# A four-layer sequence model on one core: the sorting's memory pool is opened ahead of the attention's weights, and the last element's scatters and expert tiles are given out from the second half sequence on

## The chip, the core and the metric

The kernel runs on one core of a Trainium2 chip. Such a core has five engines with an instruction queue each: TensorE (PE, matrix products), VectorE (DVE), ScalarE (ACT), GpSimd (POOL) and SyncE (SP, which here only issues DMAs). The metric is the device time of one execution in microseconds; the time of a kernel is the median of its runs.

## The reference, cut to what matters

Input x has 4 batch elements of 1024 tokens with 128 features. Four layers of two sublayers each are applied, and every sublayer is followed by `layernorm(x + sublayer(x))`. The change touches the border between the second sublayer of layer 2 and the first of layer 3, so these and their neighbours matter:

```python
x = norm(x + L2_attn(x))   # causal linear (cosformer) attention, 16 heads of 64
# L2_ffn: 8 experts, the best 2 of each token
probs = softmax(x @ router_w.T); weights, indices = top_k(probs, 2)
y = (silu(x @ w13[..., :256]) * (x @ w13[..., 256:])) @ w2      # per expert
x = norm(x + sum over the 2 chosen of weight * y)
# L3_attn: a Mamba block, 256 channels, 16 states
h = exp(delta * A) * h + delta * x * B_t ; y_t = sum over the states of h * C_t
x = norm(x + ...)
# L3_ffn: 8 experts, all computed, gated by a top-p mask
x = norm(x + sum over the 8 of gate * (relu(x @ W1 + b1) @ W2 + b2))
```

Everything is in float32.

## The kernel before, in words

The kernel is written in a framework that takes a traced program, gives each instruction a priority by its place in the program, and lets a planner order the instructions of each engine at compile time: when an engine is free in the planner's own account of time, it gets the ready instruction of the highest priority. So the order in the program is a wish, and the order on each engine is fixed once compiled. Within a pool, tiles of the same name share a number of buffers. Pools are opened and closed like a stack, on the left or the right side of on-chip memory; a pool that lies on memory of a closed pool waits for that pool's last accesses.

The parts of the program are Python generators that are stepped in turn.

- The cosformer attention (`l2_attn`) goes through 128 units: 4 batch elements x 4 quarters of 256 tokens x 8 head pairs. Its work tiles are in the pool `cos` (left), its weights in `w2` (right). The order of PE's instructions is the program's own there.
- After the last quarter of an element, `l2_dispatch` routes its 1024 tokens and sorts them by expert: it counts on DVE (its tiles are in the pool `moed`), then yields "put" and gives out 16 scatters on POOL (L1410, `xrows<-xN,di`), each of 128 token rows into a DRAM buffer. The destinations `di` and weights `wt` are in another pool, `moek`.
- `l2_ffn` is one generator, called `moe` where it is stepped. It runs over 92 tiles, 23 for each of the 4 elements, in a software pipeline: rows are loaded 8 tiles ahead (`xg`, L1469), the tile's expert weights 4 ahead (`wx`, L1485), then come the two products (`ph` or `pa_m<-xgT,wx` and `py<-wx,mh`). Before it takes up a tile whose element has not all its scatters given out, the whole pipeline is held with empty steps. When an element's last tile is through, `l2_combine` gathers the two results of each token with 16 gathers on POOL (L1556, `yg<-yrows,di`), adds and norms.
- For the last element (3) the attention's loop has ended when its sorting is done, so its 16 scatters remain as the generator `rest`.
- `l3` goes through 8 half sequences ("halves", 512 tokens each; halves 0 and 1 are element 0). Each half has a preparation (`l3_prepare`), a scan over the 16 states (`l3_scan`), and a finish. For each state, SP loads two rows broadcast to all partitions (`bn`, `cn`, L1871), POOL multiplies (`db`, L1876), ACT takes an exponential (`da`, L1880), DVE scans (L1881), POOL multiplies again (`hc`, L1892) and PE sums over the states (`pys`). For elements 1 to 3 a part of the sums is done by an accumulating DMA from POOL's queue. Half 0 is prepared during the attention, in the pool `first` and in memory that is free there. `l3` opens the pools `ssm` and `ssm2` on the left; bn, cn, db and hc are tiles of `ssm2`, with 4 buffers each.
- Between the states, `l3` gives out: a step of `rest`, a step of `moe` (two in half 0), and 3 or 4 steps of `work`, the final MoE (`l3_experts`) of earlier halves, whose weights `wh` and hidden tiles `hh` (L2007) are in the pool `top` (right). The scan's instructions are traced with a raised priority.

On the right side, pools are opened in this order: `moek`, `first`, `moet` (the tiles of `l2_ffn`), `w2`, then `moed`; `w2` and `moed` close after the attention, and `top` opens in their place.

Of the kernel before, what the change touches and what calls it, by code (L numbers as in the profile page):

```python
# [19 lines left out]
B, T, D = 4, 1024, 128  # L20
# [31 lines left out]
def weave(*gens):  # L52

    gens = list(gens)
    while gens:
        for g in gens[:]:
            if next(g, gens) is gens:
                gens.remove(g)
# [13 lines left out]
class Net:  # L72
# [1355 lines left out]

    def l2_ffn(self, wp):

        units = [
            dict(st=st, j=j, n=min(4, NT2 - j // 4 * 4))
            for st in self.m2["st"]
            for j in range(NT2)
        ]
        n = len(units)
        side = []
        for t in range(-8, n + 4):  # L1440
            while t + 8 < n and "put" not in units[max(t + 8, 0)]["st"]:
                for g in side[:]:
                    if next(g, self) is self:
                        side.remove(g)
                yield
            if 0 <= t + 8 < n and units[t + 8]["j"] % 4 == 0:
                self.l2_load_rows(units[t + 8], units, t + 8, wp)
            if 0 <= t + 4 < n:
                self.l2_weights(units[t + 4], wp)
            if 0 <= t + 2 < n:  # L1450
                self.l2_load_tile(units[t + 2], units, t + 2, wp)
            if 0 <= t < n:
                self.l2_hidden(units[t], wp)
            if 0 <= t - 2 < n:
                u = units[t - 2]
                self.l2_expert_out(u, units, t - 2, wp)
                if u["j"] == NT2 - 1:
                    side.append(self.l2_combine(u["st"], wp))
            for g in side * 2:
                if next(g, self) is self and g in side:  # L1460
                    side.remove(g)
            yield
        for g in side:
            yield from g
# [157 lines left out]
    def l3(self, moe, fp):  # L1622

        c3 = self.c3
        halves = [dict(b=b, h=h) for b in range(B) for h in range(2)]
        for i, u in enumerate(halves):
            u["prev"] = halves[i - 1] if u["h"] else None  # L1630
        halves[0] = dict(self.c3["first"], **{k: halves[0][k] for k in ("prev",)})
        for i, u in enumerate(halves[1:], 1):
            u["prev"] = halves[i - 1] if u["h"] else None
        work = self.l3_experts(fp)
        end = iter(())
        for i, u in enumerate(halves):
            nxt = iter(())
            if i + 1 < len(halves):
                if halves[i + 1]["h"] == 0:
                    while "done" not in self.m2["st"][halves[i + 1]["b"]]:  # L1640
                        next(moe)
                nxt = self.l3_prepare(halves[i + 1])
            u["final"] = i + 1 == len(halves)
            scan = self.l3_scan(u)
            for n in range(NST):
                with self.tc.high_priority(offset=1000):
                    next(scan)
                    next(end, None)
                    next(nxt, None)
                for k in range(1):  # L1650
                    next(self.m2["rest"], None)
                next(moe, None)
                if i == 0:
                    for k in range(1):
                        next(moe, None)
                for k in range(4 if n % 8 == 7 else 3):
                    next(work)
                for v in c3["todo"]:
                    v["age"] += 1
            for f in chain(scan, end, nxt):  # L1660
                pass
            end = chain(self.l3_sum(u), self.l3_finish(u))
        for f in end:
            next(work)
        c3["all"] = True
        for f in work:
            pass
# [530 lines left out]
def program(tc, io):  # L2198
    with ExitStack() as ctx:
        n = Net(ctx, tc, io)  # L2200
        wd, w0 = ExitStack(), ExitStack()
        wdp = wd.enter_context(tc.tile_pool(name="wd", bufs=1))
        W = n.l0_load(w0.enter_context(tc.tile_pool(name="w0", bufs=1)))
        d = n.l1_ffn_load(wdp)
        dp = ctx.enter_context(
            tc.tile_pool(name="rows", bufs=2, space=bass.MemoryType.DRAM)
        )
        sd = ctx.enter_context(tc.tile_pool(name="ssmd", bufs=2, space=bass.MemoryType.DRAM))
        with ExitStack() as ff:
            last = n.front(ff, w0, W, d, dp)  # L2210
            keep = ctx.enter_context(tc.tile_pool(name="moek", bufs=1, side="right"))
            first = ctx.enter_context(tc.tile_pool(name="first", bufs=1, side="right"))
            mt = ctx.enter_context(tc.tile_pool(name="moet", bufs=2, side="right"))
            w2 = ExitStack()
            n.l2_attn_load(w2.enter_context(tc.tile_pool(name="w2", bufs=1, side="right")))
            weave(*last)
        wd.close()
        def load():
            n.l2_ffn_load()
            n.l3_load(sd)  # L2220
            n.l2_rows(keep, md, dp)

        moe = n.l2_ffn(mt)
        with w2:
            md = w2.enter_context(tc.tile_pool(name="moed", bufs=1, side="right"))
            n.l2_attn(load, n.l2_dispatch, moe, first)
        n.l3_pools(ctx)
        fp = ctx.enter_context(tc.tile_pool(name="top", bufs=2, side="right"))
        n.l3(moe, fp)
# [17 lines left out]
```

## Time and profile before

| | before |
|---|---|
| runs, median (lowest to highest) | 2261.67 us (2253.73 to 2262.74), 3 runs |
| the profiled execution: time, span | 2265.2 us, 2263.4 us |
| mean granted TensorE clock | 0.934 |
| PE, DVE, ACT, POOL busy | 1988.1, 1361.8, 1184.6, 1025.0 us |
| busy in the attention's last stretch, 1200 to 1297 us: PE, DVE, POOL | 83.40, 53.87, 35.58 of 97.00 us |
| first and last scatter of element 3 issued | 1344.8, 1366.1 us |
| first and last product `db` of the scans | 1363.5, 2110.7 us |
| first matmul of the final MoE | 1525.2 us |
| after the last scan, 2126.8 to the end: PE busy | 124.30 of 136.60 us |

The span runs from the first to the last instruction of the profiled execution; its time is a little longer. Times of events below are from the span's start. A busy PE need not be PE at its peak, since matmuls are pipelined, and "granted clock" is the share of full speed at which TensorE ran.

### The profile page before, as it was taken

What the parts mean: (1) busy time and instruction counts of PE and PEld (TensorE: products, weight loads), DVE (VectorE), ACT (ScalarE), POOL (GpSimd) and SP (SyncE); (2) the same over time, 40 slices, a digit from 0 to 9 for tenths busy, and PEclk for the clock granted to TensorE, in tenths of its full rate; (3) what the DMA queues carried; (4) which work ended last, traced back from release to release, by engine and by line L of the source; (5) the groups of instructions that cost most, each with busy time, mean ns of one, the idle gap of its engine ahead of it and who ended that gap; (6) DMA issues with size and microseconds to landing.
All of it is one profiled execution on the core that took longest, in us unless ns stands there. A gap on an engine that the chain in (4) does not pass through costs nothing.

```text
span 2263.4 us, 46328 instructions
## 1 busy us (share of the span) xinstructions
PE 1988.1 (88%) x17791; PEld 1392.3 (62%) x17791; DVE 1361.8 (60%) x3705; ACT 1184.6 (52%) x2578; POOL 1025.0 (45%) x813
## 2 busy tenths in 40 slices
PE   6778889899999999999979866688898999999998
PEld 3565555544577777787768654356565656565666
DVE  7767644433455654754555555696877688686522
ACT  6532434322344444454555556476768787676443
POOL 5100411000123244234143339989788889789400
PEclk9778979889999999999999987799999999999999
DMA  3010110050000000031222066466776676676421
GB/s 107 0 38 10 31 38 1 23 172 0 2 3 2 14 27 22 25 91 41 78 79 81 17 193 193 127 193 191 205 209 172 185 186 190 181 203 170 113 61 52
DMA packets 138605, 211.04 MB, mean 93 GB/s; under 512 B 18645, under 2 KB 75982, under 8 KB 137999
## 3 DMA queue, kind: packets, MB, share of 16 engines
q1 hardware_dynamic: 126238, 173.81, 25.4%
q0 software_dynamic: 12144, 34.26, 7.3%
q8 instruction: 140, 2.29, 0.4%
q14 instruction: 83, 0.67, 0.1%
HBM read 160.22 MB, written 23.16 MB: 81 GB/s over the span
## 4 chain that ended last, share of the span: by engine, by line
PE 44%; DVE 13%; ACT 10%; issue 3%; DMA 2%; POOL 1%; SPq 0%; DVEq 0%; ACTq 0%; POOLq 0%
PE py L140 8%; PE ph L140 7%; PE po L1153 5%; DVE db L1881 5%; PE pa_m L140 5%; PE pqk L140 5%; PE kp_mo L140 3%; PE pr L1223 2%; PE pys L140 2%; PE pv L140 2%; PE pt L144 1%; ACT da L1880 1%; ACT hh L2007 1%; PE kp_mo L144 1%; ACT xN L187 1%
## 5 line engine op out<-in xcount | busy, mean ns | idle before, releaser
L1086 POOL TENSOR_TENSOR qt<-r_q,sb_c_turn 128x256 f32<-128x256 f32 (+1 forms) x256 | 164.7, 664 | 451.0 <-ACT r_q L1078 447.1
L1892 POOL TENSOR_TENSOR hc<-db,cn 128x1024 f32<-128x1024 f32 x128 | 319.0, 2529 | 67.4 <-PE pys L140 26.8
L140 PEld LDWEIGHTS py<-wh,hh 128*128 128x128 f32 x2048 | 257.0, 196 | 79.8 <-issue 47.8
L1876 POOL TENSOR_TENSOR db<-ud,bn 128x1024 f32<-128x1024 f32 x112 | 293.1, 2679 | 7.6 <-ACT dl L1841 5.1
L140 PE MATMUL ph<-xT,wh 128*128 128x512 f32 x512 | 252.9, 611 | 24.0 <-ACT hh L2007 6.7
L140 PE MATMUL py<-wh,hh 128*128 128x128 f32 x2048 | 263.8, 280 | 10.8 <-ACT hh L2007 4.2
L2007 ACT ACTIVATE hh<-ph,sb_cols 128x512 f32<-128x512 f32 x256 | 170.3, 681 | 118.3 <-PE ph L140 92.1
L1144 DVE TENSOR_TENSOR a<-pa_m,sb_c_near 128x256 f32<-128x256 f32 x256 | 96.7, 419 | 201.4 <-PE pa_m L140 201.4
L1101 ACT ACTIVATE kN<-kp_mo,sb_c_trig 128x128 f32<-128x128 f32 x448 | 130.2, 372 | 130.6 <-PE kp_mo L144 122.4
L1880 ACT ACTIVATE da<-dl,aneg 128x512 f32<-128x512 f32 x224 | 153.6, 689 | 74.4 <-DVE db L1881 73.7
L140 PE MATMUL pys<-hc,sb_c_ident 128*128 128x512 f32 x324 | 160.6, 625 | 21.3 <-POOL hc L1892 17.9
L1881 DVE TENSOR_TENSOR_SCAN db<-da,carry,db 128x512 f32<-128x512 f32 x128 | 156.9, 1265 | 21.5 <-POOL db L1876 11.2
L1881 DVE TENSOR_TENSOR_SCAN db<-da,db 128x512 f32<-128x512 f32 x128 | 149.4, 1206 | 11.5 <-ACT da L1880 6.4
L140 PEld LDWEIGHTS ph<-xT,wh 128*128 128x128 f32 x512 | 88.0, 194 | 104.3 <-issue 49.0
L2032 DVE SCALAR_TENSOR_TENSOR h_acc<-py,gt,h_acc 128x128 f32<-128x128 f32 x252 | 70.8, 343 | 123.7 <-PE py L140 123.7
L140 PE MATMUL pqk<-xT,wE 128*128 128x256 f32 x512 | 136.4, 389 | 8.2 <-ACT coT L1220 4.2
L140 PEld LDWEIGHTS pys<-hc,sb_c_ident 128*128 128x128 f32 x324 | 61.1, 201 | 83.8 <-issue 57.7
L140 PEld LDWEIGHTS pqk<-xT,wE 128*128 128x128 f32 x512 | 88.5, 193 | 21.9 <-DVE cv L1063 8.1
L1220 ACT COPY coT<-pt 128x512 f32<-128x512 f32 x64 | 37.5, 587 | 116.8 <-PE pt L144 116.8
L140 PE MATMUL po<-ht,wD 128*128 128x512 f32 x192 | 92.9, 594 | 0.0
L1153 PE MATMUL po<-cv,a 128*64 128x65 f32 x2048 | 88.3, 228 | 0.0
L1556 POOL DMA_INDIRECT yg<-yrows,di x64 | 61.3, 957 | 57.5 <-DVE ch L1388 36.7
(463 smaller groups left out, 4255.2 us busy)
## 6 DMA issues: line engine op xcount, KB each, us to landing
wx<-in_wF SPq DMA_DIRECT2D x92, 384.0 KB, 3.4
bn<-rows SPq DMA_DIRECT2D x128, 256.0 KB, 4.7
cn<-rows SPq DMA_DIRECT2D x128, 256.0 KB, 4.2
wh<-in_wH SPq DMA_DIRECT2D x64, 512.0 KB, 3.8
hc<-hc POOLq DMA_DIRECT2D x47, 512.0 KB, 7.0
xrows<-zero SPq DMA_DIRECT2D x4, 1472.0 KB, 12.0
xg<-xrows SPq DMA_DIRECT2D x20, 256.0 KB, 3.6
yrows<-ys SPq DMA_DIRECT2D x20, 256.0 KB, 3.4
```

The lines of the kernel that those rows point to most:

```text
L140: return self.nc.tensor.matmul(out=out, lhsT=lhsT, rhs=rhs, start=start, stop=stop)
L1086: nc.gpsimd.tensor_mul(u["qt"][:, m, a:], u["q"][:, a:], c2["turn"][:, m, o + a : o + 2 * P])
L1101: self.nc.scalar.activation(u["kN"][:, c, m, :], pk[:, c, :], AF.Copy, scale=trig[:, k, m : m + 1])
L1144: nc.vector.tensor_mul(u["a"][:, i, :, :], pa[i], self.c2["near"][:, None, :].to_broadcast([P, 2, P]),)
L1153: self.nc.tensor.matmul(out=u["po"][self.HALF[j], i, c, :], lhsT=lhsT, rhs=rhs, start=key not in u["begun"], stop=True, skip_group_check=True,
L1556: nc.gpsimd.indirect_dma_start(out=yg[h][:, k, c, :], out_offset=None, in_=st["out"][:, :], in_offset=bass.IndirectOffsetOnAxis(ap=st["des ...
L1876: nc.gpsimd.tensor_mul(db, ud, bc[0])
L1880: nc.scalar.activation(da, dl[:, ec, :], AF.Exp, scale=aneg[:, j : j + 1])
L1881: nc.vector.tensor_tensor_scan(db[:, ec, :], da, db[:, ec, :], carry[:, ec, n : n + 1] if h else 0.0, ALU.mult, ALU.add,)
L1892: nc.gpsimd.tensor_mul(hc, db, bc[1])
L2007: nc.scalar.activation(ht, ph, AF.Relu, bias=self.col("h_b1", i=e * NK + k))
L2032: nc.vector.scalar_tensor_tensor(acc[:, c, :], py[:, c, :], gt[:, c, e : e + 1], acc[:, c, :], ALU.mult, ALU.add,)
```

## The change

It has two parts. The pool `moed` is opened before `w2` and not after it, so that on the right side it lies next to `moet`; both still close together after the attention. And `l2_ffn` now goes through its tiles in two pipelines, one for elements 0 to 2 (69 tiles) and then one for element 3 (23 tiles), so that only the second one is held for element 3's scatters; these are given out one per state in halves from the second on, no longer in the first. The step that drains `moe` before a new element's first half tolerates its end.

```diff
--- before.py
+++ after.py
@@ -1428,11 +1428,14 @@
 
     def l2_ffn(self, wp):
 
-
+        yield from self.l2_tiles_of(0, B - 1, wp)
+        yield from self.l2_tiles_of(B - 1, B, wp)
+
+    def l2_tiles_of(self, b0, b1, wp):
 
         units = [
             dict(st=st, j=j, n=min(4, NT2 - j // 4 * 4))
-            for st in self.m2["st"]
+            for st in self.m2["st"][b0:b1]
             for j in range(NT2)
         ]
         n = len(units)
@@ -1638,7 +1641,7 @@
             if i + 1 < len(halves):
                 if halves[i + 1]["h"] == 0:
                     while "done" not in self.m2["st"][halves[i + 1]["b"]]:
-                        next(moe)
+                        next(moe, None)
                 nxt = self.l3_prepare(halves[i + 1])
             u["final"] = i + 1 == len(halves)
             scan = self.l3_scan(u)
@@ -1647,7 +1650,7 @@
                     next(scan)
                     next(end, None)
                     next(nxt, None)
-                for k in range(1):
+                if i:
                     next(self.m2["rest"], None)
                 next(moe, None)
                 if i == 0:
@@ -2212,6 +2215,7 @@
             first = ctx.enter_context(tc.tile_pool(name="first", bufs=1, side="right"))
             mt = ctx.enter_context(tc.tile_pool(name="moet", bufs=2, side="right"))
             w2 = ExitStack()
+            md = w2.enter_context(tc.tile_pool(name="moed", bufs=1, side="right"))
             n.l2_attn_load(w2.enter_context(tc.tile_pool(name="w2", bufs=1, side="right")))
             weave(*last)
         wd.close()
@@ -2222,7 +2226,6 @@
 
         moe = n.l2_ffn(mt)
         with w2:
-            md = w2.enter_context(tc.tile_pool(name="moed", bufs=1, side="right"))
             n.l2_attn(load, n.l2_dispatch, moe, first)
         n.l3_pools(ctx)
         fp = ctx.enter_context(tc.tile_pool(name="top", bufs=2, side="right"))
```

## Prediction

> **What bounds the kernel now.** I read the page first (engine shares, slices), then a table by stage, then the instruction timelines of SP, VectorE (DVE), ScalarE (ACT) and GpSimd (POOL) around the hand-over from the cosformer attention to the Mamba block, since both edits land there. The page says that TensorE (PE) carries the kernel and that POOL is heavy in the last 40%:
>
> ```profile
> PE 1988.1 (88%) x17791; PEld 1392.3 (62%) x17791; DVE 1361.8 (60%) x3705; ACT 1184.6 (52%) x2578; POOL 1025.0 (45%) x813
> PE   6778889899999999999979866688898999999998
> POOL 5100411000123244234143339989788889789400
> PEclk9778979889999999999999987799999999999999
> ```
>
> From slice 26 on (1471 us) PE is near 90% to the end. In the three slices before it, 1301 to 1471, it has its hole: 60%, and the granted clock falls with it. The table by stage (span, then busy PE, PEld, DVE, ACT, POOL, then clock, DMA share, GB/s) cuts that hole:
>
> ```profile
> 1318.00:1345.00 27.00, 16.19 (x104) 15.09 (x104) 15.72 (x70) 13.15 (x38) 7.88 (x9) 0.82 0.57 157
> 1345.00:1363.50 18.50, 5.89 (x30) 4.54 (x31) 7.68 (x22) 9.15 (x19) 14.23 (x15) 0.68 0.88 316
> 1363.50:1452.30 88.80, 59.45 (x188) 32.95 (x189) 57.45 (x81) 52.77 (x113) 82.62 (x43) 0.78 0.51 152
> 1452.30:1526.00 73.70, 59.92 (x259) 38.69 (x258) 65.15 (x112) 47.66 (x94) 67.04 (x33) 0.91 0.57 174
> ```
>
> PE is busy 16.19 + 5.89 + 59.45 + 59.92 = 141.5 of 208 us: 66.5 us idle. In half 0 (1363.5 to 1452.3) POOL is busy 82.6 of 88.8: the scan's two multiplications per state, on POOL, are the bound. The hole ends at 1525.15, when PE gets its first matmul of the final MoE (ph<-xT,wh); that needs half 0 scanned, normed and routed.
>
> Now who starts the scan. The timelines (start, us, engine, line, what; idle before and its releaser in brackets):
>
> ```profile
> 1317.47 1.12 DVE L191 TENSOR_SCALAR xN<-cr,ln_mv,ln_rs 128x128 f32<-128x128 f32 x4
> 1319.34 0.31 ACT L1754 ACTIVATE sq<-xN 128x128 f32<-128x128 f32 x1
> 1344.50 0.24 DVE L1404 TENSOR_TENSOR wt<-wt,sm 128x8 f32<-128x8 f32 x2
> 1344.82 0.33 SPq L1871 DMA_DIRECT2D bn<-rows  x1
> 1334.69 1.00 POOL L1556 DMA_INDIRECT yg<-yrows,di  x1 [36.74 <-DVE ch L1388]
> 1344.77 0.99 POOL L1410 DMA_INDIRECT xrows<-xN,di  x1 [0.30 <-DVE wt L1404]
> 1363.52 2.37 POOL L1876 TENSOR_TENSOR db<-xT,bn 128x1024 f32<-128x1024 f32 x1
> 1366.06 1.00 POOL L1410 DMA_INDIRECT xrows<-xN,di  x1 [0.17 <-issue]
> 1374.24 0.99 POOL L1556 DMA_INDIRECT yg<-yrows,di  x1 [0.16 <-DVE xc L1792]
> ```
>
> The scan's row loads (bn) go out 0.1 us after the last read of `sm`, a tile of the sorting's pool (`moed`), though the rows were written at 1270.76 and their operand at 1297. The pool `ssm2`, with bn, lies on memory of `moed` and waits for the whole of it. `ssm`, which doesn't, begins with sq at 1319.34, as soon as the attention's last read of its own pool (xN<-cr, until 1318.6) is over. Then POOL serves 15 of element 3's 16 scatters before its first multiplication.
>
> **The pool.** `top`, opened next to `moet` after the attention, holds 3 x 4 + 6 x 2 + 2 x 2 + 2 = 30 KB per partition, `moed` about 9 (two 2 KB router tiles and small ones): with `moed` opened first, it lies wholly under `top`, and `ssm2` meets only the pools of the attention and its weights, both read for the last time by 1318.6. So bn goes out at about 1319.3 instead of 1344.8 and lands 4.7 us later (its median): first multiplication possible at 1324. `top` (wh, hh) now waits for the sorting, about 1345 or, with the scan's DVE work mixed in, 1360; its first use is 140 us later: nothing, unless a wh load stands on SP ahead of bn loads and holds them; at most the 4 states loaded ahead, 4 x 4.7 = 19 us, are cover. The earlier position moves the attention's weights by 9 KB; they are loaded at 451 and first read at 585.8: nothing, and 130 us of cover.
>
> **The scatters.** 16 at 1.27 us from start to start (0.97 + 0.30) = 20.3 us leave the place before the scan and go to half 1, one per state. The first multiplication moves from 1363.5 to 1324: 39.5 us. Something is late next. Eight gathers of element 1 (1334.69 to 1344.5, 10 us), which ran on an idle POOL, now lie inside half 0: 29.5 left. Element 2's tiles are no longer held for element 3's scatters, so its first eight gathers (1520 before; 10 us) may fall in half 0 too; counting steps, they are given out at state 12 of 16. I take half: 25 us, bounds 19.5 and 29.5. So half 0 ends near 1427 and the final MoE starts near 1500 instead of 1525.
>
> **What PE pays.** PE's time is saved only where it idled. Four of element 3's 23 tiles ran in the hole (1504 to 1520); all 23 now come in halves 2 and 3, by the step count, where PE had no idle time over 3.4 us. A tile is 1.13 + 0.61 us: 4 x 1.74 = 7.0 us. In half 1 the scatters slow the scan: some 11 of 16 before 1500, 14 us of POOL, 3 states, whose sums (1.88 us each on PE) move behind: 5.6 us. Half 1 is otherwise POOL-bound as before, 67.0 of 73.7. Element 3's results are gathered in half 4 instead of 3 and needed before half 6: nothing. Sum: 25 - 7.0 - 5.6 = 12.4 us. The profiled execution took 2265.2 us (span 2263.4), 3.5 above the median of 2261.67: 2265.2 - 12.4 = 2252.8, and on the median 2249.
>
> One rule speaks against half 1. Half 0 ran at a granted clock of 0.78 with gaps of 9.5 and 5.8 us before sums; half 1 at 0.91 with element 2's and 3's tiles as filler. In half 1 no such tiles remain, so I leave PE's durations there as in half 0, which the 66.5 us already contain. The Trainium skill, "TensorE: Matmul & The Clock Gate" (Why this matters for your kernels), says that an idle gap over some 3 us drops the clock to half; by that alone the sums of half 1, some 19 us at full speed, would take up to twice as long, an estimate from the page, and the gain would be nearly nothing.
>
> **The rivals.**
> (a) POOL gives it all back: no change. From 1334.7 to half 2's first multiplication at 1539.5 POOL is rarely idle: 30.5 us of gathers, 20.3 of scatters, about 31 x 2 x 2.35 = 146 of products, 197 of 205. The same work started at 1324 ends 10.7 us earlier at best, and if element 2's last eight gathers (1549) come forward, 0.7 us. If halves 1 and 2 rather than the start of the final MoE set PE's work, the gain is 0 to 10 us: 2252 to 2262. For it: the sum. Against: after 1539 PE, not POOL, is the fuller engine.
> (b) Slower: the planner, which placed all 16 scatters into the first POOL gap, though one is given out per state, puts them in half 0 again, between products, as soon as their indices exist. Half 0 then holds 20.3 us more; with element 2's gathers the start moves 19.5 - 20.3: nothing gained, and element 3's tiles still stand in program order behind half 1: the 7.0 us and up to 7 more tiles' worth of crowding in halves 2 and 3 (12.2 us) are lost. Between +8 and +20; I take +12, 2274 on the median. It decides once more than 25 - 12.6 = 12 us of scatters slip into half 0. Against: products are given a higher priority and POOL had only 3.6 us of gaps inside half 0.
> (c) More: scatters and gathers fall into POOL's gaps of halves 2 to 4 (it is busy 87.5 of 103.9 us in half 2), half 0 shifts the full 29.5, and nothing is lost on PE: 2232.
> (d) The change misses: bn still waits, for another tile of the sorting or the load queue, and only the scatters go: 1363.5 to about 1350, 13 us, less 12.6: no change, 2262.
>
> **How the numbers follow.** A measurement of this kernel can tell about 0.5%, 11 us, from no change; 2249 lies just beyond it. My sum with its bounds and (c) get 0.56 together, of which some 0.05 lie within 11 us; (a) and (d) 0.25, of which 0.03 beyond it; (b) 0.19, nearly all beyond. So faster 0.54, same 0.28, slower 0.18. The range reaches from a little under (c), since waits on wx loads (19.8 us in the hole, with DMA at 316 GB/s while scan rows, wh and wx load together) may also shrink, to just short of (b): 2228 to 2271.
>
> **What would show it.** Right: bn issued near 1319, not after the last read of `sm`; the first product near 1324; no scatter before it; the final MoE's first matmul near 1500; half 2 beginning at 1530 to 1540; PE idle in the hole near 54 us. Wrong: scatters between products of half 0 (rival b); a final MoE that starts early while PE in half 1 is under 60% busy and halves 2 and 3 take longer than 104 and 113 us (a); bn after 1340 (d). If the time differs while everything up to the first product is as told, my account of PE is wrong.

## The result: 40 us slower, and the profile after

| | before | after |
|---|---|---|
| median of the runs | 2262.2 us (2253.73 to 2266.24, 4 runs) | 2302.4 us (2300.59 to 2303.98, 4 runs) |
| ratio, 95% interval | | 1.0179 [1.0159, 1.0199] |
| span and clock of the profiled execution | 2263.4 us, 0.934 | 2299.7 us, 0.926 |

The forecast was 2249 us, with a range up to 2271. The page of the changed kernel, engine shares and slices, against the first fence of the prediction:

```profile
PE 2001.6 (87%) x17791; PEld 1400.2 (61%) x17791; DVE 1374.2 (60%) x3705; ACT 1181.0 (51%) x2574; POOL 1025.7 (45%) x813
...
PE   6778889899899999999879866679898989898998
...
POOL 5100401000233243243233179898896869878500
PEclk9778879899999999999999968879999999899999
```

The instructions are the same in number, and PE is busy 13 us longer for them. Its hole is still three slices wide, and behind it there are slices at 8 where before had 9. The order of events at the hand-over, from the instruction timelines of SP, POOL and DVE (start, us, engine, line, what; idle before and its releaser):

```profile
1320.28 0.33 SPq L1874 DMA_DIRECT2D bn<-rows  x1
...
1323.87 2.35 POOL L1879 TENSOR_TENSOR db<-xT,bn 128x1024 f32<-128x1024 f32 x1 [24.22 <-DMA bn<-rows]
...
1362.81 0.24 DVE L1404 TENSOR_TENSOR wt<-wt,sm 128x8 f32<-128x8 f32 x2
1367.35 1.00 POOL L1410 DMA_INDIRECT xrows<-xN,di  x1 [0.17 <-issue]
...
1419.22 1.00 POOL L1410 DMA_INDIRECT xrows<-xN,di  x1 [0.17 <-issue]
```

bn no longer waits for the sorting: it goes out 42 us ahead of the last read of `sm`, and the first product is at 1323.87, where the forecast had 1324. But all 16 scatters, which the program gives out from half 1 on, run from 1367 to 1419, between half 0's products, which end with half 1's first product at 1443.2.

The tables by stage (start and end, length, busy PE, PEld, DVE, ACT, POOL with instructions, clock, DMA share, GB/s) of halves 1 to 6 before, which the prediction did not show beyond 1526:

```profile
1452.30:1539.50 87.20, 73.42 (x344) 48.91 (x343) 73.19 (x129) 57.28 (x117) 79.61 (x40) 0.92 0.59 178
1539.50:1643.30 103.80, 90.02 (x465) 60.22 (x463) 78.14 (x151) 77.39 (x155) 87.39 (x47) 0.98 0.72 204
...
1756.00:1850.70 94.70, 88.69 (x440) 57.75 (x439) 73.66 (x144) 75.46 (x142) 81.63 (x42) 0.99 0.67 182
...
1940.90:2036.10 95.20, 89.99 (x443) 60.11 (x442) 72.97 (x139) 64.09 (x114) 82.15 (x42) 0.97 0.71 186
```

and after, from half 0 on:

```profile
1323.90:1443.20 119.30, 77.58 (x321) 53.86 (x321) 87.06 (x164) 67.19 (x154) 101.65 (x62) 0.76 0.61 187
1443.20:1549.70 106.50, 69.53 (x217) 37.75 (x216) 77.11 (x135) 68.30 (x128) 91.79 (x51) 0.81 0.46 136
1549.70:1641.30 91.60, 82.28 (x394) 53.18 (x393) 70.16 (x123) 64.26 (x123) 79.71 (x40) 0.98 0.63 169
...
1755.10:1874.00 118.90, 103.81 (x510) 69.78 (x511) 77.13 (x155) 82.83 (x166) 96.90 (x56) 0.95 0.65 176
...
1968.60:2077.00 108.40, 98.84 (x458) 62.63 (x457) 73.91 (x135) 69.54 (x121) 81.10 (x41) 0.92 0.63 166
```

Length less busy PE gives PE's idle time. From 1318 to half 0's end it fell from 52.8 to 43.4 us. In half 1 it rose from 13.8 to 37.0. Half 4 adds 9.1 (15.1 against 6.0) and half 6 adds 4.4; the 9.4 us up to half 0's end and 4.0 us over the other halves go against these. From 1318 to the end PE is idle 152.3 us against 129.1, 23.2 more, as much as half 1 lost. With the 13.1 us that PE is busy longer, this is the whole 36.3 us between the two spans.

The counts of matmuls show that work was displaced rather than done early. By the end of half 2, which comes at about the same time (1643.3 before, 1641.3 after), PE had issued 1131 matmuls before and 962 after since 1318 (after with the 30 ahead of half 0). By the end of half 4, with half 3's 491 and 587, the counts are level (2062 and 2059), but at 1850.7 before and at 1874.0 after. (Some records are missing from every trace, so such counts are good to a few per cent.)

What half 1 lost, in its groups of PE instructions (out<-in, count, busy us, mean ns of one, idle before and its releasers). Before:

```profile
L140 PE MATMUL pys<-hc,sb_c_ident 128*128 128x512 f32 x59 | 27.7, 594 | 0.0
L140 PE MATMUL ph<-xgT,wx 128*128 128x128 f32 x112 | 17.2, 303 | 0.9 <-ACT ys L1537 0.9
L140 PE MATMUL py<-wx,mh 128*128 128x128 f32 x56 | 9.5, 298 | 1.3 <-DVE th L1928 1.3
```

After:

```profile
L140 PE MATMUL pys<-hc,sb_c_ident 128*128 128x512 f32 x64 | 35.9, 702 | 14.6 <-POOL hc L1895 11.5 <-DVE xs L1920 3.2
...
L140 PE MATMUL ph<-xgT,wx 128*128 128x128 f32 x38 | 6.0, 309 | 4.3 <-DMA wx<-in_wF 4.3
L140 PE MATMUL py<-wx,mh 128*128 128x128 f32 x28 | 4.6, 296 | 0.0
```

A tile has eight ph products. Before, half 1 held 14 tiles: element 2's last seven (1460 to 1495) and element 3's first seven (1504 to 1537). After, it holds five, the last of element 2, whose `ph` products start in its first 16 us (1443 to 1458); element 2's other two have moved into half 0, and element 3's begin at 1619, in half 2. The products of tiles fell from 26.7 to 10.6 us. The sums, `pys`, have nothing between them, and one costs 702 instead of 594 ns at a clock of 0.81 instead of 0.92. The worst wait, in the timelines of PE and POOL:

```profile
1463.16 1.88 PE L140 MATMUL pys<-hc,sb_c_ident 128*128 128x512 f32 x4
1468.19 3.67 PE L140 MATMUL pys<-hc,sb_c_ident 128*128 128x512 f32 x8 [3.15 <-DVE xs L1920]
1483.35 3.76 PE L140 MATMUL pys<-hc,sb_c_ident 128*128 128x512 f32 x4 [11.48 <-POOL hc L1895]
1486.92 1.97 PE L140 MATMUL po<-sb_s_e,xs 128*128 128x128 f32 x16
...
1530.81 2.08 PE L140 MATMUL ph<-xT,wh 128*128 128x512 f32 x2
```

```profile
1471.19 0.99 POOL L1559 DMA_INDIRECT yg<-yrows,di  x1
...
1479.98 0.94 POOL L1559 DMA_INDIRECT yg<-yrows,di  x1 [0.30 <-issue]
1480.93 4.66 POOL L1895 TENSOR_TENSOR hc<-db,cn 128x1024 f32<-128x1024 f32 x2
```

Eight gathers of element 2, whose tiles are now done early, stand ahead of two second products of half 1. PE's queue stands at the sum that needs one of them; behind it is `po`, half 0's output projection, with half 0's whole finish. So the final MoE starts at 1530.8, 5.7 us later than before, though half 0's scan ended 9 us earlier.

### The profile page after: what moved, and what is told of

The parts are those of the page before. It is cut to its first block, busy times and chain, and to the rows that moved or that the text cites. A ratio compares the mean times of both kernels' runs of the same rounds, so it can differ in the third digit from the quotient of the medians.

```text
span 2299.7 us, 46335 instructions
## 1 busy us (share of the span) xinstructions
PE 2001.6 (87%) x17791; PEld 1400.2 (61%) x17791; DVE 1374.2 (60%) x3705; ACT 1181.0 (51%) x2574; POOL 1025.7 (45%) x813
## 4 chain that ended last, share of the span: by engine, by line
PE 41%; DVE 16%; ACT 9%; issue 3%; POOL 2%; DMA 2%; SPq 0%; POOLq 0%; DVEq 0%; ACTq 0%
PE py L140 7%; PE ph L140 6%; DVE db L1884 6%; PE po L1153 5%; PE pqk L140 5%; PE pa_m L140 4%; PE kp_mo L140 3%; PE pv L140 2%; PE pr L1223 2%; PE pys L140 2%; PE pt L144 1%; PE kp_mo L144 1%; ACT hh L2010 1%; DVE xc L1795 1%; ACT L177 1%
## 5 line engine op out<-in xcount | busy, mean ns | idle before, releaser
L1879 POOL TENSOR_TENSOR db<-ud,bn 128x1024 f32<-128x1024 f32 x112 | 283.0, 2589 | 42.2 <-DVE ud L1843 42.2
L140 PE MATMUL ph<-xT,wh 128*128 128x512 f32 x512 | 261.5, 624 | 30.2 <-ACT hh L2010 7.1
L1884 DVE TENSOR_TENSOR_SCAN db<-da,db 128x512 f32<-128x512 f32 x128 | 149.0, 1205 | 12.6 <-ACT da L1883 5.8
L140 PE MATMUL pa_m<-r_q,r_k 64*64 64x128 f32 x2048 | 86.8, 285 | 0.0
## 6 DMA issues: line engine op xcount, KB each, us to landing
xrows<-zero SPq DMA_DIRECT2D x4, 1472.0 KB, 11.6
```

The lines of the kernel that those rows point to most:

```text
L140: return self.nc.tensor.matmul(out=out, lhsT=lhsT, rhs=rhs, start=start, stop=stop)
L1879: nc.gpsimd.tensor_mul(db, ud, bc[0])
L1884: nc.vector.tensor_tensor_scan(db[:, ec, :], da, db[:, ec, :], carry[:, ec, n : n + 1] if h else 0.0, ALU.mult, ALU.add,)
```

## Experiments

The theories: **A**, the order of the tiles (element 2's and 3's tiles leave half 1, and PE has nothing to do there); **B**, the scatters between half 0's products; **C**, element 2's gathers ahead of half 1's second products; **D**, preparations of the next half that come late. Each set of runs has its own runs of the kernel before, and ratios are to these. The kernel before ran at 2294.0 and 2298.0 us in the first and second set, and at 2257.9 and 2259.4 in the third and fourth, which is about where the result was taken (2262.2): so ratios are compared within a set, and across sets only where the text says so. Times in the table are from the start of the attention's last product with its weights (`wE`), so that they don't hold what differed ahead of it; a half ends with the next half's first product.

| set, kernel | ratio [95%] | half 0 ends | half 1 ends | final MoE starts | end |
|---|---|---|---|---|---|
| result: before | 1 | 139.4 | 226.6 | 212.2 | 950.5 |
| result: after | 1.0179 [1.0159, 1.0199] | 128.6 | 235.0 | 216.2 | 985.0 |
| 1: pool alone | 0.9931 [0.9906, 0.9956] | 128.8 | 226.3 | 211.4 | 954.1 |
| 1: split and late scatters, no pool | 1.0099 [1.0074, 1.0124] | 159.6 | 250.1 | 208.5 | 997.3 |
| 1: pool and split | 1.0024 [1.0012, 1.0036] | 129.3 | 234.4 | 215.5 | 974.3 |
| 1: pool and late scatters | 1.0046 [1.0025, 1.0068] | 129.2 | 209.6 | 186.4 | 970.3 |
| 2: before | 1.0000 [0.9986, 1.0015] | 150.0 | 237.1 | 222.8 | 964.3 |
| 2: after | 1.0088 [1.0060, 1.0117] | 127.9 | 234.5 | 215.7 | 984.8 |
| 2: two pipelines woven | 1.0090 [1.0060, 1.0121] | 128.4 | 230.8 | 228.0 | 988.2 |
| 2: pool, no scatters of element 3 | 0.9914 [0.9886, 0.9942] | 126.0 | 218.0 | 198.5 | 947.1 |
| 3: after, scatters tied to half 1 | 1.0113 [1.0089, 1.0136] | 121.6 | 230.7 | 214.4 | 974.6 |
| 3: after, gathers tied to half 2 | 1.0153 [1.0129, 1.0176] | 129.0 | 218.9 | 198.8 | 973.5 |
| 3: after, element 2's tail in half 1 | 1.0294 [1.0268, 1.0321] | 128.0 | 220.3 | 191.1 | 1005.7 |
| 3: after, preparation early | 1.0259 [1.0235, 1.0284] | 142.0 | 241.9 | 238.7 | 1004.8 |
| 4: after | 1.0194 [1.0166, 1.0222] | 128.1 | 234.5 | 215.6 | 985.1 |
| 4: pool alone | 1.0009 [0.9992, 1.0026] | 128.9 | 225.1 | 211.6 | 946.1 |
| 4: pool and split | 1.0130 [1.0102, 1.0158] | 128.3 | 234.7 | 215.8 | 968.2 |
| 4: after, both ties | 1.0145 [1.0110, 1.0180] | 120.9 | 215.2 | 180.5 | 972.0 |

### Set 1: the parts one by one

**Pool alone.** The kernel before, with only this line moved:

```diff
             w2 = ExitStack()
+            md = w2.enter_context(tc.tile_pool(name="moed", bufs=1, side="right"))
...
         with w2:
-            md = w2.enter_context(tc.tile_pool(name="moed", bufs=1, side="right"))
```

> The pool moed opened ahead of w2 alone; one pipeline of 92 tiles and the scatters given out in half 0, as before the change. Theory A (the loss of 40 us comes from the order of the tiles: with two pipelines, element 3's tiles come only from half 2 on, and PE idles 37 us in half 1 instead of 14): no loss here, element 3's tiles run in half 1 again and half 0 still ends some 9 us earlier; 2245 to 2262 us. Theory B (the loss comes from the pool: scatters and gathers now lie between the products of half 0, which takes 119 instead of 89 us, and delays the rest): the loss is here, 2285 to 2305 us. The order of POOL's instructions in half 0 is the same as in the changed kernel, so half 0 should take 115 to 120 us in both theories.

**Split and late scatters, without the pool.** The changed kernel, with the same line moved back.

> The two pipelines and the late scatters alone; moed opened after w2 as before the change. Theory A: slow, PE idles in half 1 as in the changed kernel, 2285 to 2310 us. Theory B: about as before, 2255 to 2270 us. In both the scan rows go out at 1345 us again and the 16 scatters stand in one gap ahead of the products, since the planner hoists them.

**Pool and split.** The changed kernel with the scatters given out from half 0, as before:

```diff
-                if i:
+                if True:
                     next(self.m2["rest"], None)
```

> The changed kernel with element 3's scatters given out from half 0 on again; two pipelines, moed ahead. Theory A, if the holding back of the tiles comes from the split itself (the first pipeline is drained to its last gather before the second starts, and that one takes 8 empty steps to its first tile): as slow as the changed kernel, 2295 to 2310 us, first tile of element 3 still after 1600 us. If it comes from the late scatters: 2245 to 2265 us. Theory B: 2295 to 2310 us.

**Pool and late scatters.** The changed kernel with one pipeline over all tiles:

```diff
-        yield from self.l2_tiles_of(0, B - 1, wp)
-        yield from self.l2_tiles_of(B - 1, B, wp)
+        yield from self.l2_tiles_of(0, B, wp)
```

> The changed kernel with one pipeline of 92 tiles; the scatters late, moed ahead. Element 2's last 8 tiles then wait in program order for element 3's scatters as well. Theory A: slow, 2290 to 2320 us, with PE idle in half 1 at least as long as in the changed kernel. Theory B: 2295 to 2310 us. Here the two theories agree; the run shows whether the late scatters cost time without the split.

Measured: 0.9931, 1.0099, 1.0024 and 1.0046. The expected times go with a kernel before at 2262 us, which ran at 2294 here, so they are to be read as ratios. The pool alone is then in theory A's range, and the second kernel just under A's and above B's. The third lies between its ranges and the fourth below both of its: these two missed. In this set the pool gains, and what loses is the other half of the change. With the scatters given out from half 0 or from half 1, the planner puts them between the same products of half 0; so theory B alone can't tell pool alone (0.9931) from pool and split (1.0024). With one pipeline, the late scatters cost 1.15% over the pool alone (1.0046 less 0.9931), a little more than the split did. There element 2's last eight tiles come after them as well: they run at 1538 to 1598, and element 3's at 1607 to 1759.

### Set 2: place of the tiles against scatters

**Before and after, unchanged**, for the base and for traces of this set.

> The kernel before, unchanged, profiled beside the others: on the chip of the four runs above its time was 2294 us, 32 us above the profiled chip's, while a kernel close to the changed one took 2300 there as here. If the chip as a whole is slower, every stage is longer by about 1.4%; if it is the hand-over, half 0 or half 1 alone is longer. Both theories: ratio 1.000.

> The changed kernel, unchanged, beside the others on one chip. From the pool alone (0.9931) and the order alone (1.0099) the product is 1.003, the kernel with early scatters gave 1.0024, and the first comparison 1.0179. If the two parts simply add: 1.000 to 1.008. If the first comparison holds on every chip: 1.016 to 1.020.

**Two pipelines woven.** Pool and split, with the second pipeline stepped beside the first one's tail, which was to give element 3's tiles their old place:

```diff
-        yield from self.l2_tiles_of(0, B - 1, wp)
-        yield from self.l2_tiles_of(B - 1, B, wp)
+        last = self.l2_tiles_of(B - 1, B, wp)
+        for f in self.l2_tiles_of(0, B - 1, wp):
+            yield
+            if "put" in self.m2["st"][B - 1]:
+                next(last)
+        yield from last
```

> Two pipelines and moed ahead as in the changed kernel, but the scatters are given out from half 0 on and the second pipeline is stepped beside the first one's tail, not after it: element 3's first tile has its place in state 8 of half 1 again, as before the change, and element 2's tiles are not held. Theory A (the tiles' order): element 3's tiles start near 1510 us, PE idles 20 us or less in half 1, and the time is that of the pool alone or less, a ratio of 0.985 to 0.996. Theory B (products, scatters and gathers mixed in half 0): POOL's order in half 0 is the same as in the changed kernel, so a ratio of 1.00 to 1.02.

**No scatters of element 3.** Pool alone, without that work:

```diff
             for k in range(2):
+                if b == B - 1:
+                    yield
+                    continue
                 i = nc.gpsimd.indirect_dma_start(
```

> The pool alone, and element 3's 16 scatters are left out (its tiles then work on rows of zeros; everything else is computed). It prices the scatters in half 0. If POOL bounds half 0, that half is 20 us shorter (98 instead of 118 us), the final MoE starts 15 to 20 us earlier, and the time is a ratio of 0.983 to 0.989, 10 to 20 us below the pool alone. If PE's tiles decide alone: the time of the pool alone, 0.991 to 0.995.

The woven kernel missed: 1.0090, no better than the changed one. Element 3's tiles came to 1536 to 1695, nearer to their old place (four start in half 1, against seven before), but element 2's tail still lay early (it starts its last tile at 1473, 15 us into half 1), so half 1 stayed short of tiles. Its stage, and the wait of PE that the gathers of element 2 make in it:

```profile
1457.60:1559.90 102.30, 67.58 (x245) 38.24 (x244) 73.90 (x132) 62.20 (x122) 89.34 (x49) 0.83 0.49 151
```

```profile
PE pys L140 <- POOL hc L1899: 11.5, 1, 11.5
```

34.7 us of idle PE, and the same 11.5 us. So element 3's place is not enough; the tail of element 2 is the other part of theory A, which I had left out, and theory C came from this wait. The kernel without element 3's scatters, 0.9914, is no better than the pool alone in the set before it (0.9931): half 0 ends 2.8 us earlier and the end comes 7.0 us earlier. The expected 20 us off half 0 are not there. Scatters among half 0's products are not what costs 40 us.

The base itself taught something. In this set the kernel before ends half 0 10.6 us later after the attention than in the set of the result (150.0 against 139.4), while the changed kernel keeps its 128. So part of the gain of pool alone in set 1 could be that kernel's loss in half 0. This is why set 4 repeats it. The changed kernel's 1.0088 lies outside both of its expected ranges, a little above the sum of the parts.

### Set 3: one stall at a time

**Scatters tied.** Each scatter of element 3 waits for the second product of one state of half 1:

```diff
+            self.hold = nc.gpsimd.tensor_mul(hc, db, bc[1]).ins
...
-                if b < B - 1:
-                    self.tc.add_manual_dep(i, self.beat.name, SYNC, reason="spread out")
+                last = self.beat if b < B - 1 else self.hold
+                self.tc.add_manual_dep(i, last.name, SYNC, reason="spread out")
```

> The changed kernel with each of element 3's 16 scatters tied to the second product of one state of half 1, so that they cannot come between half 0's products; this is the placement that the prediction's sum assumed. The changed kernel itself stood at 1.009 of the kernel before in its repeat. If the scatters in half 0 are the cause (theory B): half 0 is 15 to 20 us shorter than the changed kernel's 119 us, the final MoE starts about 15 us earlier, and the ratio falls to 0.998 to 1.003. If the order of the tiles is the cause (theory A): half 1 keeps some 35 us of idle PE and now carries the 20 us of scatters as well, and the ratio stays at 1.005 to 1.014.

**Gathers tied.** Element 2's combine is given out from half 2 on, each gather waiting for that half's latest second product:

```diff
+    def l2_held(self, st, wp):
+        while self.m2["half"] < 2:
+            yield
+        yield from self.l2_combine(st, wp)
...
+                if b == 2:
+                    self.tc.add_manual_dep(g, self.hold.name, SYNC, reason="held")
```

> The changed kernel with element 2's 16 gathers tied to half 2's products, out of half 1 where eight of them stood ahead of a second product. Theory C (these gathers make PE's queue stand at a sum of half 0 for 11.5 us, and with it half 0's output projection and the final MoE): that wait is gone, half 1 falls from 106 to about 90 us, the final MoE starts about 15 us earlier, the ratio falls from 1.009 to 1.000 to 1.004. Theory A (PE has no tiles of elements 2 and 3 to run in half 1): half 1 gets shorter on POOL, but what is saved comes back in halves 2 to 4: 1.006 to 1.011.

**Element 2's tail in half 1.** The first pipeline is held ahead of its last eight tiles:

```diff
-            while t + 8 < n and "put" not in units[max(t + 8, 0)]["st"]:
+            while (t + 8 < n and "put" not in units[max(t + 8, 0)]["st"]) or (
+                b1 < B and t + 8 == n and self.m2.get("half", 0) < 1
+            ):
...
         for i, u in enumerate(halves):
+            self.m2["half"] = i
```

> The changed kernel with element 2's last eight tiles held until half 1, where the kernel before ran them; element 3's tiles still come from half 2 on. Theory A: half 1's idle PE time falls from 37 to 20 to 25 us and its clock rises from 0.81 to 0.88 or more; half of the loss is regained, ratio 1.000 to 1.004. Theory B (scatters between half 0's products): nothing changes in half 0, 1.007 to 1.011. Theory D (late preparations): only by chance, since the preparations' steps are the same.

**Preparation early.**

```diff
                     next(nxt, None)
+                    next(nxt, None)
```

> The changed kernel with the preparation of the next half given out two steps per state instead of one. Theory D (POOL waits 42 us in all at the starts of halves for ud, the preparation's last tile, where the kernel before waited 5 us for its preparation): these waits fall under 15 us and the ratio falls from 1.009 to 0.995 to 1.001. Theory A (those waits are only the place where PE's displaced tiles show): the waits move to other instructions, and the ratio stays within 1.004 to 1.012.

The expected ratios had taken 1.009 as the changed kernel's own; this set's base is that of the result, so they are to be read against 1.018 to 1.019.

Tied scatters: 1.0113, some 0.7% better. Half 0 ends 7 us earlier than in the changed kernel, not 15 to 20, and half 1 keeps 36.8 us of idle PE (109.1 long, 72.25 busy). By its ratio B is a part, by its stages A stays. Tied gathers: 1.0153, some 0.3% better, but the intervals overlap. The 11.5 us are gone (they stood at a sum of half 1, not of half 0 as the expectation says) and half 1 is 90.0 us long and ends 15.6 us earlier than in set 4's changed kernel; 11.6 us of it arrive at the end. C is at most a small part.

Element 2's tail: half 1 came right, and the time went wrong, 1.0294. Its stages of half 1 and half 5, and POOL's waits for the preparation over the scans (us in total, times, longest):

```profile
1440.50:1532.80 92.30, 80.26 (x309) 45.37 (x310) 73.01 (x130) 61.06 (x117) 81.89 (x40) 0.89 0.49 155
...
1849.50:1996.70 147.20, 105.11 (x474) 65.88 (x474) 83.72 (x169) 88.34 (x167) 96.96 (x56) 0.85 0.49 133
```

```profile
POOL db L1882 <- DVE ud L1846: 70.3, 2, 41.1
```

Idle PE in half 1 fell to 12.0 us at a clock of 0.89, so the tail is what was missing there, as theory A says. At half 3's end this kernel is 26 us ahead of the kernel before. But element 3's tiles now run from 1687 to 1878 and its gathers from 1901, inside half 5. Half 6, whose input is element 3, has its preparation behind them: its first product waits 41.1 us, and 42.1 us of PE stand idle in half 5. (The other wait, 29.2 us, is that of half 5's first product.) Here the early half 1 was lost again to the late element 3.

Preparation early: 1.0259, worse. POOL's waits for the preparation over the scans, first of the changed kernel and then of this one (us in total, times, longest):

```profile
POOL db L1879 <- DVE ud L1843: 42.2, 4, 20.1
```

```profile
POOL db L1880 <- DVE ud L1844: 18.1, 2, 15.4
POOL db L1880 <- DVE prl L1257: 14.8, 1, 14.8
POOL db L1880 <- ACT dl L1845: 8.8, 1, 8.8
```

They moved and kept their sum (41.7 us), and half 0, into which the preparation's steps now come, grew to 132.9 us. The ratio lies outside the ranges of D and of A. D is not borne out; that those waits are only the place where a late PE shows fits this, but is not shown.

### Set 4: the shares against one base

Kernels a1, e1b and e3b are the changed kernel, pool alone, and pool and split again; the fourth has the ties of the scatters and of the gathers together.

> The changed kernel again, as the base of this set. At the quicker level of the kernel before (2258 to 2262 us) 1.016 to 1.020, at the slower level (2294 to 2298 us) 1.006 to 1.012.

> The pool's move alone, again. If its gain is a property of the kernel: 0.990 to 0.996 at either level. If the kernel before lost some 11 us in half 0 in the first set by chance of the level (its half 0 took 100 us there instead of 89), which the early start avoids: 0.999 to 1.005 at the quicker level.

> The pool and the split of the tiles into two pipelines, scatters given out from half 0 as before. Theory A (order of the tiles): 0.007 to 0.012 above the pool alone. The rest up to the changed kernel, 0.004 to 0.007, is then the late giving out of the scatters. If the split cost nothing and the level made the difference: within 0.003 of the pool alone.

> The changed kernel with both ties: element 3's scatters one per state of half 1, element 2's gathers in half 2. If the two stalls add up: 0.009 below the changed kernel (1.007 to 1.010 at the quicker level), with half 0 near 112 us and no wait of 11 us for a second product in half 1. What then remains above the pool alone is the price of element 3's late tiles (theory A). If half 1 is bound by its missing tiles alone: no better than the tied scatters, 1.010 to 1.013.

The shares come from the medians of this set: pool alone 2261.87 against 2259.36, nothing that can be measured; the split 24.9 us more (2286.74); the late scatters 15.4 us more (2302.13). Together 42.8 us, 1.94%. These are shares in this order; on one pipeline, in set 1, the late scatters cost 1.15%, so the two parts overlap. The pool's gain in set 1 is then most likely the loss of that set's kernel before, for which there is no profile; set 2's, at the same level, lost 10.6 us in half 0. No version here beats the kernel before at both levels: the pool alone is as fast as it at one, and 0.7% faster at the other.

The pool alone, halves 0 and 1:

```profile
1313.10:1432.70 119.60, 76.70 (x298) 51.47 (x296) 86.39 (x163) 66.67 (x150) 101.66 (x63) 0.76 0.61 187
1432.70:1528.90 96.20, 82.05 (x337) 50.35 (x338) 76.25 (x131) 61.67 (x122) 84.19 (x43) 0.84 0.54 166
```

From the attention's end, its first product comes 41.3 us earlier than before (9.3 against 50.6), half 0's end 10.5, half 1's end 1.5. POOL is busy 101.66 us in half 0 instead of 82.62: gathers and scatters that ran ahead of the first product now lie among the products.

Half 1 and half 6 of the pool and split, and half 6 of the changed kernel in this set:

```profile
1443.50:1549.90 106.40, 70.17 (x217) 37.66 (x216) 77.16 (x135) 68.45 (x128) 91.73 (x51) 0.81 0.44 136
...
1966.90:2058.90 92.00, 86.15 (x428) 56.10 (x427) 73.09 (x138) 64.14 (x114) 82.10 (x41) 0.99 0.73 193
```

```profile
1968.60:2078.10 109.50, 98.94 (x458) 62.68 (x457) 73.91 (x135) 69.68 (x121) 81.06 (x41) 0.92 0.61 163
```

The split alone empties half 1: PE is idle 36.2 us in it, against 14.2 with the pool alone. The same 22.1 us part the two kernels at the end (968.2 and 946.1 in the table), as theory A has it. The late scatters leave all this as it is: halves 0 and 1 end, and the final MoE starts, within 0.2 us of the pool and split. Their cost comes behind half 1. Element 3's first tile starts at 1620 instead of 1600, and half 6 takes 109.5 us instead of 92.0, though it starts at nearly the same time. Part of this stands at its end: half 7's first product waits 15.2 us on POOL for `ud`, the last tile of its preparation, where in the pool and split it waits 5.1 us for an operand from ACT. What makes that preparation late stays open.

Both ties: every sign that I listed as right came true. Half 0 has no scatters, half 2 begins at 1531.0, the final MoE starts at 1496.28; from the attention's end that is 31.7 us earlier than before. And the time is 1.0145, slower by 30 us in the medians and above both expected ranges. Its halves 1 and 2:

```profile
1436.60:1531.00 94.40, 74.06 (x286) 43.10 (x285) 69.81 (x115) 58.34 (x104) 86.67 (x45) 0.86 0.45 139
1531.00:1644.00 113.00, 87.92 (x373) 54.65 (x372) 76.22 (x151) 69.56 (x141) 97.86 (x59) 0.87 0.58 165
```

Idle PE in these two is 20.3 and 25.1 us, against 13.8 and 13.8. Element 3's tiles start at 1607; the final MoE of half 0, begun early, is not enough to fill half 2.

## Why the prediction was wrong

**The start of the scan: right.** bn at 1320.28 and the first product at 1323.87, as worked out from the memory of the pools. Nothing took the place of that wait.

**The scatters leave half 0: wrong.** The planner put all 16 between half 0's products, which is rival (b)'s mechanism. My reason against it, POOL's 3.6 us of gaps in half 0, was read from a half 0 that began late. Length less busy time is 6.2 us there, and 17.7 us in the one that begins early (119.30 less 101.65).

**25 us at half 0's end and at the final MoE: wrong in size, and then in worth.** Measured 9.1 at half 0's end, and the final MoE 5.7 us late. The scatters' 20.3 us on POOL were worth less than their sum: half 0 ended 7.0 us earlier when they were tied to half 1, and 2.8 us earlier when they were left out. With both ties the final MoE did start early enough, by 31.7 us, and the kernel still lost 30 us. The start of the final MoE is not what sets the end: five kernels of the table start it before 199 us, and four of these are slower than the kernel before. The fifth is the one without element 3's scatters, where element 3's tiles have nothing to wait for.

**What PE pays, 12.6 us: the step that failed.** I counted four displaced tiles of element 3. I wrote that in half 1 "no such tiles remain" and then left PE's durations there as in half 0, "which the 66.5 us already contain". They don't: the 66.5 us are idle time that was left with 14 tiles in half 1. I had also seen that element 2's tiles are no longer held, but drew from it only the earlier gathers. Half 1 lost 23.2 us of idle PE, and at the lower clock its sums alone took 6.9 us more. Set 4 gives the prices: 24.9 us for the split, whose half 1 is emptied in the same way, and 15.4 us for the late scatters, behind half 1, where my sum had "nothing" for element 3's later results. Together they are 40.3 us, where my sum had 12.6; and the gain of 25 us that stood against them is nothing that can be measured in the pool alone. Why half 1's loss isn't regained is read from the stages and not tested by itself. From half 2 on PE is near 90% busy, so there is little room for tiles that come later: halves 4 and 6 are 24.2 and 13.2 us longer than before, and half 2 12.2 us shorter. With the final MoE pulled forward in their stead half 2 ran dry. How the late scatters lengthen half 6 stays open.

**Rival (a) was right for the pool.** Its sum, POOL's work from 1334.7 to half 2, gave 10.7 us at best and perhaps 0.7; measured on the pool alone were 1.5 us at half 1's end and 1.0009 in time. Had I let this sum stand against the 25 us, the base of the forecast would have been no gain at all, and only the costs would have been left.

**Rival (b) was right about the place of the scatters and short in its price**, +12 against +40: it counted the scatters and the crowding in halves 2 and 3, not half 1. The pool alone has the scatters between the same products and loses nothing, so their place isn't the cause of the loss.

**Element 3's gathers "needed before half 6: nothing".** In the changed kernel they run from 1812, in half 4, and in set 4 half 6 starts only 1.7 us later than in the pool and split; but half 6 itself is longer there. The cover is one half: with the gathers at 1901, half 5 took 147.2 us.

**The clock.** "TensorE: Matmul & The Clock Gate" of the Trainium skill (Why this matters for your kernels) spoke against half 1, and the trace agrees in kind. Four sums took 3.76 us right after the wait of 11.48, and 1.88 at 1463.16: exactly twice. But the eight sums at 1468.19 followed a gap of 3.15 us and took 3.67 us, the full rate. Over the half the loss is smaller than the rule by itself would make it, since most sums don't follow such a long gap: 702 against 594 ns, 64 x 0.108 = 6.9 us. (The prediction set out from some 19 us of sums in half 1; before, they took 27.7.)

Two more things stay open. Why the kernel before has two levels, 1.5% apart, is not known; it isn't the chip alone, since sets 1 and 3 ran on one chip and sets 2 and 4 on another, each with one set of either level. And the ties gave 0.7% and 0.3% singly, against the result's ratio, but 0.5% together (1.0194 less 1.0145); the intervals overlap, and why the two don't add up is not known.

## What to carry to other kernels

When a change takes filler work out of a stage that another engine bounds, price the emptied stage. Here 16 us of filler left half 1, its idle time on PE grew by 23 us, and the granted clock there was 0.81 instead of 0.92. (The clock doesn't go by the idle time alone: the pool alone had 0.84 with 14.2 us idle.) An earlier start is worth what the bounding engine's total work lets through (41.3 us at the first product were 1.5 us at half 1's end), so sum that engine's work over the stages behind before counting a gain on any single event. And a step that is given out later in the program moves everything held behind it, also the steps that it used to hold back.

## What the runs showed of the hardware that I had not expected

The same kernel on one core ran at 2258 to 2262 us in two sets and in the result, and at 2294 to 2298 in two others. In the second set's profile the attention ended 12.8 us later than in the result's, and half 0, which begins right behind it, took 100.0 instead of 88.8 us. The changed kernel's half 0 took 118.7 and 119.3 us. In every profile of the first and second set, whatever the kernel, the attention's last product with its weights started at 1321 to 1331 us, and in the others at 1304 to 1316; behind it the changed kernel took the same 985 us in all three of its profiles. So the same change is 1.018 to 1.019 at one level and 1.009 at the other, and the pool alone 1.001 or 0.993: a verdict of under 1% has to be repeated in another set.
